# A gated GNN kernel: TensorE transposes of h and y replaced by VectorE block transposes and an exchange through DRAM

## The chip, the cores and the metric

The kernel runs as one program on one core of one Trainium2 chip. The metric is the device time of that program in microseconds (us). The engines named below are TensorE (PE, with its weight loads PEld), VectorE (DVE), ScalarE (ACT), GpSimd (POOL) and SyncE (SP, which here only issues DMAs). POOL issues DMAs too; POOL's go through queue q0, SP's through queue q1, and both feed the same 16 DMA engines.

## What is computed

There are 16 graphs of 1024 nodes with 128 features each, and an adjacency matrix `adj` of 1024 x 1024 zeros and ones for each. Two layers run one after the other, cut here to what matters:

```python
h = maximum(layernorm(x), 0)                       # y: per node, over the 128 features
for i in range(4):                                 # layer 0: gated
    m = einsum('bjn,bjd->bnd', adj, h @ weight[i])
    gx = m @ w_ih[i].T + b_ih[i];  gh = h @ w_hh[i].T + b_hh[i]
    r = sigmoid(xr + hr); z = sigmoid(xz + hz); n = tanh(xn + r * hn)
    h = (1 - z) * n + z * h
x = x + h * nodemask
h = maximum(layernorm(x), 0)
for i in range(4):                                 # layer 1: graph convolution with batch norm
    h = relu(einsum('bnm,bmc->bnc', adj, h @ W[i]) + b[i])
    h = batchnorm over all graphs and nodes (h)
out = x + h
```

## The kernel before

The program has two stages: a gated stage (layer 0, all graphs) and a convolution stage (layer 1, all graphs). A slower general path stands behind a flag that the exact path computes; it does not run here.

**Layout.** In the gated stage h lives transposed: features on the 128 partitions, nodes along the free axis, in halves of 512 nodes (`hf`). Gates and weights work on that layout. The aggregation needs the other one: nodes on the partitions, since it sums over source nodes. It takes h as a high part (rounded to fp32r) and a low part (the rest), so each aggregation multiplies two parts with the rows of `adj`, 32 matmuls of 512 columns (`aggregate_rows`, L521, matmul at L525).

**Turning by TensorE.** `split_step` (L741) makes the two parts. In layer 0 they come from `y`, which has nodes on the partitions already (`split_high`, `split_low`). In layers 1 to 3, `features_times` (L491) transposes h on TensorE, eight blocks of 128 x 128 into PSUM (L498, tile `hw_g`); ACT copies the high part out (L502) and DVE subtracts it for the low part (L503). Two more turns are on TensorE: `turn` (L639) turns y into the first h of a graph (L647, tile `pt_in`, copied out by ACT at L648), and `tail_norm` (L651) turns the last h back to nodes (L657, tile `pt_x`), which DVE adds to x (L660) before it takes the sums of the next layer norm (L609, L610). A nested function `rest` (L675) applies that norm on ACT (L625) and stores y for the convolution stage.

**Two streams and half-steps.** Stream A takes the even graphs and stream B the odd ones. `half_step(one, two)` (L856) lets stream `two` compute its gates (`gate_step`, L781, twice: for each half, six fp32 matmuls at L790, sigmoid, two DVE operations, tanh, sigmoid, three DVE operations) while stream `one` splits its h and then aggregates. The main loop (L997) calls it with the streams in turn, 60 times. Eight half-steps, a cycle, take a pair of graphs through the four layers. In the text they are numbered HS0 to HS7: in an even one A aggregates layer 0, 1, 2, 3 in turn (HS0, HS2, HS4, HS6) and B computes gates; in an odd one the roles are exchanged. B's gates of layer i run while A aggregates layer i+1.

After the aggregation ACT copies its two PSUM halves to `m` (L770); the next half-step's gates need h first (`g_r<-h`, one matmul) and then `m` (`g_r<-m`). The four gate results have one PSUM bank each (`g_r`, `g_hn`, `g_xn`, `g_z`), so the matmuls of the second half wait until ACT and DVE have read those of the first.

**Beside that** each graph needs, in the gated stage:
- its rows copied from the input to a scratch in DRAM (`copy_rows`, L572, eight DMAs of POOL), and loaded from there (`load_rows`, L577, eight DMAs of SP, called from `take` at the end of the stream's last gates);
- a check of the rows' low bits by DVE (`look`, L585), four rows at a time (`look_on`, L838);
- its rows cast to bf16 by POOL (L594) and turned by a DMA transpose of SP (L595), eight of each in one half-step (`transpose_rows`, L591), through two buffers; POOL then stores the turned matrix to `adjT_d`, laid out partition first, for the convolution stage;
- x of the graph two further on loaded and normed (`ahead`, L817): loaded by POOL when the stream is in layer 1, normed as a whole in layer 2, and turned on TensorE in layer 3.

**What sets the order.** In the start-up phase the order of all five engines is the program's own (`manual_schedule(engines=every)`). In the main loop only POOL's and SP's is (L995); PE, DVE and ACT are ordered by the framework's planner, which moves operations about, with a few `issue_after` fences (`behind`, L683). All engines execute their own instructions strictly in order. The convolution stage is ordered by the planner.

**The convolution stage** loads the turned matrices, 2-byte, in eight pieces of 256 KB for every graph and layer (`load_adjT`, L1018), widens them on DVE and ACT (L1026, L1028) and aggregates with the same L525. Odd graphs use the one large buffer (`block`), even graphs eight small ones (`packed`, tag `half`).

The functions that the change touches:

Of the kernel before, what the change touches and what calls it, by code (L numbers as in the profile page):

```python
# [16 lines left out]
P = 128  # L17
# [324 lines left out]
def exact_path(  # L342
# [42 lines left out]
    adjT_d = [dram.tile([P, NB, N], BF16, tag=f"adjT{b}", name=f"adjT_d{b}") for b in range(B)]  # L385
# [148 lines left out]
    with ExitStack() as st:  # L534
# [37 lines left out]
        def copy_rows(b):  # L572
            raws[b] = rawd.tile([N, N], F32, tag="raw", name=f"raw{b}")
            for j in range(NB):
                nc.gpsimd.dma_start(raws[b][j * P : (j + 1) * P, :], adj[b][j * P : (j + 1) * P, :])
# [8 lines left out]

        def look(b, row, j, part=0):  # L585
# [5 lines left out]
        def transpose_rows(b, row, j, adjT):  # L591

            t = work.tile([P, N], BF16, tag="half1", name=f"half{b}_{j}", bufs=2)
            nc.gpsimd.tensor_copy(t, row.bitcast(F32))  # L594
            nc.sync.dma_start_transpose(adjT[:, :, j * P : (j + 1) * P], t)  # L595

        def norm(xt, y, name):

            norm_apply(xt, y, norm_stats(xt, name))
# [39 lines left out]
        def turn(y, name, hT=None, func=AF.Copy):  # L639

            if hT is None:
                hT = work.tile([P, N], F32, tag="h", name=f"h_{name}", bufs=7)
# [8 lines left out]
        def tail_norm(b, xt, hT):  # L651

            for hf in range(NH):
                pt = tmp(f"pt_x{b}_{hf}")
                for q in range(BH):
                    k = hf * BH + q
                    nc.tensor.transpose(pt[:, q * P : (q + 1) * P], hT[:, k * P : (k + 1) * P], ident)  # L657
                for q in range(BH):
                    k = hf * BH + q
                    nc.vector.scalar_tensor_tensor(  # L660
                        xt[:, k, :],
                        pt[:, q * P : (q + 1) * P],
                        maskT[:, b * NB + k : b * NB + k + 1],
                        xt[:, k, :],
                        ALU.mult,
                        ALU.add,
                    )
# [13 lines left out]
        written = [True]  # L681

        def behind(*inss):  # L683

            es = ExitStack()
            for ins in () if written[0] else inss:
                es.enter_context(tc.issue_after(ins.ins))
            return es

        class Stream:  # L690


            def __init__(self, first):
                self.b, self.i, self.rest, self.tag = first, 0, None, "AB"[first % 2]
                self.opened = None
# [31 lines left out]
            def prepare(self, b, xt):  # L727
# [568 lines left out]
```

## Time and profile before

| what | value |
|---|---|
| time, median of 3 runs | 1842.16 us (1841.27 to 1842.33) |
| the profiled execution's own time | 1840.61 us |
| its span in the trace | 1838.8 us |
| PE busy | 1821.5 us, 99% of the span |
| DVE busy | 1225.6 us, 67% |
| ACT busy | 1035.8 us, 56% |
| POOL busy | 285.0 us, 15% |
| clock granted to TensorE | 0.999 of full speed |
| moved by DMA | 381 MB, 207 GB/s on average |

The gated stage fills the first 1,200 us or so and the convolution stage the rest. The page gives, for each engine, the time in which it executed something; a group line gives a line of the kernel, the engine, what is written from what, the count, the busy time, the mean duration of one in ns, and the idle time of the engine just ahead of the group's instructions with what ended it. In a table of windows each row is one stretch of time and gives the busy time of each engine in it. Matmuls overlap in the pipeline, so the durations of single matmuls add to more than the time they take; distances from one start to the next are the better measure.

### The profile page before, as it was taken

Reading aid. Unit: us, or ns where it says so; the run is one execution under the profiler, and the core shown is the slowest. Engines: PE = TensorE matmul, PEld = TensorE weight load, DVE = VectorE, ACT = ScalarE, POOL = GpSimd, SP = SyncE. Lnnn points to the kernel's source line nnn. Section 1 sums busy time; section 2 is a strip of 40 time slices with the busy share of each in tenths; the row PEclk is TensorE's granted clock in tenths of the full one; section 3 lists DMA queues with packets and bytes.
Section 4 is the critical chain, followed back from the end, with each engine's and each line's share of the span. In section 5 each row is a group of like instructions: output and inputs, shape, how many; then the busy total and the mean of one; then the engine's idle time right before and its main releaser. Section 6 shows DMA issues by size and latency. Waiting matters only on the chain.

```text
span 1838.8 us, 21960 instructions
## 1 busy us (share of the span) xinstructions
PE 1821.5 (99%) x7326; PEld 1254.2 (68%) x7326; DVE 1225.6 (67%) x2244; ACT 1035.8 (56%) x1577; POOL 285.0 (15%) x378
## 2 busy tenths in 40 slices
PE   9999999999999999999999999999999999999997
PEld 6566666656566666666565666667778888888886
DVE  7656667567666766766766757676666666666665
ACT  5544454553545554445355353467777767767764
POOL 4131320230231042023023013011100000000011
PEclk9999999999999999999999999999999999999999
DMA  7189775575486386567557546349876676767676
GB/s 264 39 247 317 209 229 195 162 206 192 159 233 180 126 233 178 196 172 217 218 159 206 178 145 172 103 159 332 291 248 228 212 256 204 257 209 260 210 249 242
DMA packets 256280, 381.21 MB, mean 207 GB/s; under 512 B 149932, under 2 KB 155856, under 8 KB 252320
## 3 DMA queue, kind: packets, MB, share of 16 engines
q1 hardware_dynamic: 237968, 245.95, 44.2%
q0 software_dynamic: 17664, 133.53, 20.4%
q8 instruction: 59, 0.97, 0.2%
q14 instruction: 61, 0.50, 0.1%
q10 hardware_dynamic: 528, 0.26, 0.0%
HBM read 287.39 MB, written 117.44 MB: 220 GB/s over the span
## 4 chain that ended last, share of the span: by engine, by line
PE 94%; DVE 2%; ACT 2%; issue 1%; DMA 1%; SPq 0%; POOL 0%; DVEq 0%; ACTq 0%; POOLq 0%
PE pm L525 24%; PE pc_m L525 12%; PE g_r L790 11%; PE g_z L790 11%; PE pc_g_r L525 6%; PE pc_g_z L525 6%; PE g_hn L790 6%; PE g_xn L790 6%; PE hw_c L500 4%; PE hw_g L498 2%; PE pw_g_hn L1096 1%; PE pw_g_xn L1096 1%; PE pt_in L647 1%; PE pt_x L657 1%; PE pc_g_r L510 1%
## 5 line engine op out<-in xcount | busy, mean ns | idle before, releaser
L525 PE MATMUL pm<-row,ghw 128*128 128x512 f32 x2048 | 515.6, 406 | 0.1
L525 PEld LDWEIGHTS pm<-row,ghw 128*128 128x128 f32 x2048 | 383.2, 188 | 112.6 <-issue 36.9
L525 PE MATMUL pc_m<-wide,chw 128*128 128x512 f32 x1024 | 246.0, 395 | 0.0
L525 PEld LDWEIGHTS pc_m<-wide,chw 128*128 128x128 f32 x1024 | 190.5, 188 | 42.3 <-issue 4.3
L807 ACT ACTIVATE r<-r,vecs 128x512 f32<-128x512 f32 x128 | 92.3, 721 | 216.8 <-DVE r L804 216.8
L525 PE MATMUL pc_g_r<-wide,chw 128*128 128x512 f32 x464 | 187.0, 403 | 0.3 <-ACT chw L502 0.3
L525 PE MATMUL pc_g_z<-wide,chw 128*128 128x512 f32 x464 | 180.9, 390 | 0.0
L594 POOL CAST half<-row 128x1024 bf16<-128x1024 f32 x128 | 139.7, 1108 | 250.9 <-DMA adjT<-half 169.6
L1028 DVE CAST wide<-packed 128x1024 fp32r<-128x1024 bf16 x160 | 110.0, 692 | 74.5 <-PE pc_m L525 56.4
L1028 DVE CAST wide<-block 128x1024 fp32r<-128x1024 bf16 x160 | 110.2, 691 | 73.2 <-PE pc_g_z L525 40.2
L503 DVE TENSOR_TENSOR ghw<-hw_g,ghw 128x512 fp32r<-128x512 f32 x96 | 62.0, 686 | 129.7 <-ACT ghw L502 129.5
L1026 ACT CAST wide<-block 128x1024 fp32r<-128x1024 bf16 x96 | 100.6, 1048 | 59.3 <-PE pc_m L525 34.3
L803 DVE SCALAR_TENSOR_TENSOR r<-g_hn,vecs,r 128x512 f32<-128x512 f32 x128 | 95.4, 745 | 56.8 <-ACT r L802 31.3
L1026 ACT CAST wide<-packed 128x1024 fp32r<-128x1024 bf16 x96 | 100.7, 1049 | 55.6 <-PE pc_g_z L525 23.7
L790 PE MATMUL g_r<-m,w_mT 128*128 128x512 f32 x256 | 130.7, 592 | 0.0
L790 PE MATMUL g_z<-m,w_mT 128*128 128x512 f32 x256 | 130.7, 592 | 0.0
L790 PE MATMUL g_xn<-m,w_mT 128*128 128x512 f32 x256 | 130.7, 592 | 0.0
L589 DVE TENSOR_REDUCE low<-row 128x1 f32<-128x1024 uint16 x112 | 128.6, 1210 | 0.0
L808 ACT ACTIVATE z<-g_z,brz 128x512 f32<-128x512 f32 x128 | 87.1, 680 | 71.0 <-PE g_z L790 71.0
L770 ACT COPY m<-pm 128x512 f32<-128x512 f32 x128 | 68.8, 586 | 101.3 <-PE pm L525 101.2
L802 ACT ACTIVATE r<-g_r,brz 128x512 f32<-128x512 f32 x128 | 87.7, 685 | 60.3 <-PE g_r L790 59.5
L810 DVE TENSOR_TENSOR h<-h,r 128x512 f32<-128x512 f32 x96 | 74.6, 777 | 62.4 <-ACT r L807 62.4
(176 smaller groups left out, 2764.0 us busy)
## 6 DMA issues: line engine op xcount, KB each, us to landing
packed<-adjT_d SPq DMA_DIRECT2D x256, 256.0 KB, 5.9
block<-adjT_d SPq DMA_DIRECT2D x256, 256.0 KB, 5.4
raw<-in_adj_dram POOLq DMA_DIRECT2D x112, 512.0 KB, 11.6
row<-raw SPq DMA_DIRECT2D x112, 512.0 KB, 5.8
adjT_d<-adjT POOLq DMA_DIRECT2D x16, 2048.0 KB, 7.9
xmid_d<-x POOLq DMA_DIRECT2D x16, 512.0 KB, 4.8
y<-ymid_d POOLq DMA_DIRECT2D x16, 512.0 KB, 5.1
ymid_d<-y_mid POOLq DMA_DIRECT2D x15, 512.0 KB, 3.0
```

The source lines that it names most:

```text
L500: nc.tensor.matmul(pt[:, q * P : (q + 1) * P], src, w, start=True, stop=True)
L525: nc.tensor.matmul(pm[hf], hw[s][:, j * P : (j + 1) * P], rows[j][:, hf * HALF : (hf + 1) * HALF], start=(j == 0 and s == 0), stop=(j == N ...
L589: nc.vector.tensor_reduce(low[:, k : k + 1], lows, axis=AX.X, op=ALU.max)
L594: nc.gpsimd.tensor_copy(t, row.bitcast(F32))
L790: nc.tensor.matmul(po, wT[:, i, g * C : (g + 1) * C], rhs, start=start, stop=stop)
L802: nc.scalar.activation(r, pr, AF.Sigmoid, bias=brz[:, 3 * i : 3 * i + 1])
L803: nc.vector.scalar_tensor_tensor(r, phn, b_hn(i), r, ALU.add, ALU.mult)
L807: nc.scalar.activation(r, r, AF.Tanh, bias=b_in(i))
L808: self.last_act = nc.scalar.activation(z, pz, AF.Sigmoid, bias=brz[:, 3 * i + 1 : 3 * i + 2])
L810: nc.vector.tensor_sub(ho, hin, r)
L1026: nc.scalar.copy(r, t)
L1028: nc.vector.tensor_copy(r, t)
```

## The change

Every turn of h and y in the main loop leaves TensorE. DVE transposes 32 x 32 blocks of a 128 x 512 half in one instruction, with the blocks written in an order that puts what belongs to the same destination partitions together. The 128 partitions are then exchanged in four groups of 32: SP stores the tile to a scratch in DRAM (`exchange_out`, one DMA of 256 KB with 2 KB rows) and loads it back into the same tile by four DMAs (`exchange_in`, 64 KB each, in pieces of 512 B). The result has nodes on the partitions in their own order and stays in the permuted order along the free axis; the readers use views (`nodes_of`, `four_ways`, `by_nodes`) with runs of 32 elements. Three kinds of turn go this way: h after every gate half (`gate_step`), y of the next graph (`turn_across`), and the last h of a graph, which `tail_norm` takes from the same exchanged tile. The first three splits, the turns of y of graphs 0 and 1 and the tails of graphs 14 and 15 stay on TensorE.

With it the main loop gets an order written out by hand for all five engines:
- the split (`split_part`) is put between the gates of the other stream: the ACT copy of the high part and the DVE subtraction stand ahead of the tanh of the same half, and read SBUF, not PSUM;
- the second half's load back, the turning of rows and all side work come after the gates, in fixed places (`beside_aggregation`): the tail of a graph comes half a step later than before, and the norm of x is spread over three layers;
- rows are loaded at the start of the half-step in which the stream computes its last gates (before: after them);
- casts, DMA transposes and row copies go four at a time over four half-steps (before: eight in one), and two of every four casts write to a tile of the `half` pool, which the exchange tiles use too;
- `adjT_d` is laid out block first, and even and odd graphs exchange their buffers in the convolution stage.

```diff
-    adjT_d = [dram.tile([P, NB, N], BF16, tag=f"adjT{b}", name=f"adjT_d{b}") for b in range(B)]
+    adjT_d = [dram.tile([NB, P, N], BF16, tag=f"adjT{b}", name=f"adjT_d{b}") for b in range(B)]
...
+        def exchange_out(t, name):
+            d = rawd.tile([P, HALF], F32, tag="cross", name=f"cross_{name}", bufs=6)
+            nc.sync.dma_start(d, t)
+            return d
+
+        def exchange_in(d, t):
+
+            src = d.rearrange("(t r) (s x) -> s r t x", t=4, s=4)
+            for s in range(4):
+                nc.sync.dma_start(t[s * 32 : (s + 1) * 32, :].rearrange("r (t x) -> r t x", t=4), src[s])
...
-            t = work.tile([P, N], BF16, tag="half1", name=f"half{b}_{j}", bufs=2)
+            if j % 4 < 2:
+                t = work.tile([P, N], BF16, tag="half1", name=f"half{b}_{j}", bufs=2)
+            else:
+                t = half_tile(f"half{b}_{j}")
             nc.gpsimd.tensor_copy(t, row.bitcast(F32))
             nc.sync.dma_start_transpose(adjT[:, :, j * P : (j + 1) * P], t)
...
+        def turn_across(y, name):
+
+            hT = work.tile([P, N], F32, tag="h", name=f"h_{name}", bufs=7)
             for hf in range(NH):
-                pt = tmp(f"pt_x{b}_{hf}")
+                cols = slice(hf * HALF, (hf + 1) * HALF)
+                t = half_tile(f"ty_{name}_{hf}").bitcast(F32)
+                nc.vector.transpose(
+                    t.rearrange("p (a k i) -> p k a i", a=4, i=32), y[:, cols].rearrange("p (k a c) -> p k a c", a=4, c=32)
+                )
+                exchange_in(exchange_out(t, f"{name}_{hf}"), hT[:, cols])
+            return hT
+
+        def by_nodes(cols):
+            return cols.rearrange("c (q k i) -> c k q i", q=4, i=32)
+
+        def four_ways(cols):
+            return cols.rearrange("p (k a c) -> p k a c", a=4, c=32)
+
+        def nodes_of(t):
+
+            return t.rearrange("p (a k c) -> p k a c", a=4, c=32)
...
+            def split_part(self, g):
+                if g == 0:
+                    self.hw = hw_tiles(self.b, f"ghw{self.b}_{self.i}")
+                if self.i == 0:
                     self.split_high(g)
                     self.split_low(g)
+                    return
+                hi, lo = (four_ways(t[:, g * HALF : (g + 1) * HALF]) for t in self.hw)
+                src = nodes_of(self.parts[g])
+                nc.scalar.copy(hi, src)
+                nc.vector.tensor_sub(lo, src, hi.bitcast(F32))
...
+                if self.goes_across():
+                    t = half_tile(f"th{nm}").bitcast(F32)
+                    nc.vector.transpose(t.rearrange("p (q k c) -> p k q c", q=4, c=32), four_ways(ho))
+                    self.outs.append((exchange_out(t, f"h{nm}"), t))
+                if hf == 0:
+                    self.exchange()
...
+        def turn_rows():
+
+            for b, row, j in waiting_rows[:4]:
+                if j == 0:
+                    adjTs[b] = turned_tile(f"adjT{b}")
+                transpose_rows(b, row, j, adjTs[b])
+                if j == NB - 1:
+                    nc.gpsimd.dma_start(adjT_d[b].rearrange("k p n -> p k n"), adjTs[b])
+            del waiting_rows[:4]
+            for dst, src in copies[:4]:
+                nc.gpsimd.dma_start(dst, src)
+            del copies[:4]
+
+        def beside_aggregation(one, two):
+
+            if one.b + 2 < B and one.i == 2:
+                one.next_apply()
+            if two.ends:
+                two.ends.pop(0)()
+            if one.ends:
+                one.ends.pop(0)()
+            if two.b + 2 < B and two.i == 2:
+                two.next_sums()
+            if one.b + 2 < B and one.i == 3:
+                one.next_turn()
+            one.look_on()
+
         def half_step(one, two, gated=None, halfway=None):
 
-            if one.i > 0:
+            if one.i == 1:
+                one.give_rows()
+            if two.i == L - 1 and two.b + 2 < B:
+                two.next_rows = load_rows(two.b + 2)
+            by_turns = one.i > 0 and not one.parts
+            if by_turns:
                 one.split_step()
-            two.gate_step(0)
-            two.gate_step(1)
+            for hf in range(NH):
+                two.gate_step(hf, None if by_turns else lambda: one.split_part(hf))
             if gated:
                 gated()
-            if one.i == 0:
-                one.split_step()
+            two.exchange()
+            if two.i == 1:
+                two.ahead()
+            turn_rows()
+            beside_aggregation(one, two)
             one.agg_step(0)
...
-        with tc.manual_schedule(engines={mybir.EngineType.Pool, mybir.EngineType.SP}):
-            written[0] = False
+        with tc.manual_schedule(engines=every):
+            stage_two.append(True)
             for s in range(2, B // 2 * L):
                 half_step(sa, sb)
                 half_step(sb, sa)
+        with tc.manual_schedule(engines={mybir.EngineType.Pool, mybir.EngineType.SP}):
             sb.gate_step(0)
             sb.gate_step(1)
...
-        block = turned_tile(f"block{b}_{i}") if b % 2 else None
+        block = None if b % 2 else turned_tile(f"block{b}_{i}")
```

In the code `between` runs after a half's two first DVE operations and ahead of its tanh, and `self.parts` holds the exchanged tiles of a stream's newest h. `look_on` now looks at rows in layers 1 and 3 of stream A and 2 and 3 of stream B.

## The prediction

> **What bounds the kernel now.** I read the busy shares first, then one cycle of eight half-steps in windows, then PE's order of time, then the groups that the change touches, and last the DMAs.
>
> The page's busy line and its DMA slices:
>
> ```profile
> PE 1821.5 (99%) x7326; PEld 1254.2 (68%) x7326; DVE 1225.6 (67%) x2244; ACT 1035.8 (56%) x1577; POOL 285.0 (15%) x378
> ...
> DMA  7189775575486386567557546349876676767676
> ```
>
> PE has no room; DVE and ACT have a third and more. Windows of one cycle, about a half-step each (length, then busy time of PE, PEld, DVE, ACT, POOL, then clock, DMA share, GB/s):
>
> ```profile
> 591.10:609.50 18.40, 18.40 (x65) 11.39 (x64) 14.00 (x20) 7.13 (x13) 0.00 (x0) 1.00 0.59 210
> 609.50:628.00 18.50, 18.50 (x65) 11.40 (x64) 12.22 (x40) 10.83 (x21) 1.47 (x2) 1.00 0.42 167
> 628.00:646.40 18.40, 18.40 (x65) 11.39 (x64) 10.78 (x35) 11.06 (x20) 2.69 (x4) 1.00 0.17 57
> 646.40:665.00 18.60, 18.60 (x65) 11.40 (x64) 13.88 (x16) 7.46 (x12) 6.50 (x11) 1.00 1.01 315
> 665.00:683.40 18.40, 18.40 (x65) 11.39 (x64) 13.28 (x31) 8.02 (x15) 8.85 (x11) 1.00 0.62 124
> 683.40:704.00 20.60, 20.60 (x69) 12.08 (x68) 11.05 (x30) 13.20 (x25) 5.63 (x9) 1.00 0.95 307
> 704.00:722.50 18.50, 18.50 (x71) 11.69 (x70) 13.54 (x17) 10.16 (x18) 5.51 (x6) 1.00 0.69 182
> 722.50:741.00 18.50, 18.50 (x72) 11.85 (x71) 13.10 (x17) 6.65 (x12) 0.00 (x0) 1.00 0.39 138
> ```
>
> PE is full in every window. DVE sums to 101.9 us of 149.9, ACT to 74.5, the DMA shares to 89.6 us. So in this stage whatever leaves PE shortens the cycle, until something else is late. PE's order of time shows what leaves (start, length, instruction):
>
> ```profile
> 637.64 7.85 PE L525 MATMUL pm<-row,ghw 128*128 128x512 f32 x32
> 645.33 1.03 PE L498 MATMUL hw_g<-ident,h 128*128 128x128 f32 x8
> 646.20 1.02 PE L790 MATMUL g_r<-h_in,w_hhT 128*128 128x512 f32 x2
> 647.06 1.02 PE L790 MATMUL g_r<-m,w_mT 128*128 128x512 f32 x2
> ```
>
> From start to start eight transposes take 646.20 - 645.33 = 0.87 us and a gate matmul 0.86. A half-step without turns is 12 x 0.86 = 10.3 us of gates and 7.3 of aggregation, 17.6 us; eight are 141.
>
> **1. Turns taken off PE.** Counts from the groups:
>
> ```profile
> L498 PE MATMUL hw_g<-ident,h 128*128 128x128 f32 x384 | 50.0, 272 | 0.2 <-ACT w_mT L488 0.2
> L657 PE MATMUL pt_x<-ident,h 128*128 128x128 f32 x128 | 16.7, 272 | 0.0
> L647 PE MATMUL pt_in<-ident,y_in 128*128 128x128 f32 x128 | 16.6, 272 | 0.0
> ```
>
> Three splits of 48, two tails and two turns of y stay: 384 - 24, 128 - 16, 128 - 16, so 584 transposes go, at 0.87/8 each: **-63.5 us**, all on the path.
>
> **2. DVE transposes.** 118 for h (59 layers of graphs, two halves) and 28 for y, 20 in a cycle. No row shows one. Nearest from below: the widening cast at L1028, 1024 columns in 0.69 us, so 0.35 for 512; from above: the low-bit check at L589, 1.21 us for 1024 elements. I take 0.7, what a 128x512 DVE operation takes undisturbed (L811: 0.69). DVE's cycle becomes 102 + 14 = 116 us of 141 (126 at the upper bound): it fits, so 0.
>
> The Trainium skill, "VectorE: DVE Perf Modes", "The three transpose paths", gives 311 ns for 128x128 bf16 on VectorE and advises TensorE for a full 128x128 turn where PSUM will do, which speaks against this change. Its figure would estimate 1.24 us here and 127 us of DVE in a cycle; the price it puts on TensorE, 390 ns, is not what this trace shows as PE's cost, 0.109 us in a chain of eight. Its advice would forbid the move; the windows, with PE full and DVE not, allow it.
>
> **3. Split and tail from SBUF.** ACT's copy of the high part goes from 0.60 us (PSUM source, L502) to 0.63 (SBUF source, L753), DVE's subtraction from 0.69 to 0.70 (L757). The 28 copies of `h_in` (0.60 us) leave ACT. Hidden, since both engines have slack.
>
> **4. Order, and the copies of `m`.** The eight transposes also covered ACT's copy of `m`. Now only one gate matmul (0.86 us) does; the copy takes 0.59. With ACT free it just fits. In four half-steps of eight ACT is inside a norm (table load 1.28, root 0.30, eight activations 3.2 together), begun after the last sigmoid, about 11.2 us into the half-step, with DVE's two small operations now behind the new transpose (about 13.6): it ends at 17 to 18 us, against an aggregation that ends at 17.6. I take 0.3 us a time, 4 x 7 cycles: **+8 us** (bounds 0 and 1.2 us a time, 34).
>
> **5. The exchange.** SP stores 256 KB, waits, issues four loads, and the next half-step's split needs them. Clock from the start of a half-step: first half's sigmoid 2.6, DVE to 4.3, tanh 5, sigmoid z 5.9, three DVE operations 7.4, transpose 8.1. In the next half-step ACT wants the tile at 17.6 + 2.5 = 20.1. Late by L, it holds the tanh and the sigmoid z behind it on ACT, which PE needs to reuse bank `g_z` at 26.1 in the second half; copy, tanh and sigmoid are 2.0, so PE feels it only from 24 on: 16 us after the transpose. For the second half it is the low part, needed in mid-aggregation, with 17 us. DMA rows (issue to landing; the last line is that of L595):
>
> ```profile
> ymid_d<-y_mid POOLq DMA_DIRECT2D x15, 512.0 KB, 3.0
> x<-in_x_dram POOLq DMA_DIRECT2D x14, 512.0 KB, 6.3
> DMA to landing us min/median/max: 3.0/3.2/12.7
> ```
>
> The store: 3 us. The loads, 512 B pieces as in x: four issues at 0.32 us (SP's row of L581) and 3.7 us (a lone 256 KB of x at the start). Together 8 us, half of what is allowed. From above: while eight row copies keep the DMA engines full (646 to 662 us, share 1.0) a DMA transpose took 11.2 us to land; two in series would be 22. The copies now come four at a time, and only HS2 to HS5 have any, so I take 8 to 14 us and no wait of PE. Volume: the packet records have 84 ns for 2 KB and 27 ns for 512 B, so (128 x 84 + 512 x 27)/16 = 1.5 us an exchange, 31 a cycle: 120 of 141, 85%. In the gated stage the exchanges share q1 with the DMA transposes, 1.23 us of SP each, now four a half-step and behind the exchange.
>
> The skill's "DMA: Bandwidth & Descriptors", "Anatomy of one DMA", puts a fixed 2.0 us on each DMA and its rules say transfers under 64 KB are mostly overhead. By it store and loads would be 2.6 and about 2.6 in series, some 5 us, even less than the rows give; contention is what it leaves out.
>
> **6. Rows loaded early.** Eight loads (10 us of DMA at 159 ns per 4 KB) now stand in q1 ahead of the stores of layer 3's h. Those are wanted only by the tail, after the next gates, 13 us later; y's exchanges have two half-steps. Cover: that distance. 0.
>
> **7. POOL casts beside DVE.** DVE operations with two SBUF sources stretch while POOL casts:
>
> ```profile
> 652.88 2.73 DVE L810 TENSOR_TENSOR h<-h_in,r 128x512 f32<-128x512 f32 x1 [1.95 <-ACT r L807]
> 653.04 2.03 POOL L594 CAST half<-row 128x1024 bf16<-128x1024 f32 x2
> ```
>
> 0.69 became 2.73. The casts now come in fours and the subtraction joins the exposed operations; whether the transpose does is not shown. Per cycle the stretching costs some 5 us of DVE now; at most all 17 us of casts. Inside DVE's room; 0, with up to 1.5 us of PE in HS2 to HS5 as the upper bound, 42 us.
>
> **8. Strided gate operands.** In layer 0 of 14 graphs, 84 matmuls read h and write PSUM in runs of 32. No row has that; the nearest, the last transposes' strided weight load, takes 211 ns against 141. I take 0 (whole runs of 128 B) and 36 us as the upper end (half as slow again).
>
> **9. `adjT_d` and buffers.** A graph's store becomes 2 KB pieces, 672 ns for eight against 622 for 16 KB: 0.4 us of DMA a graph, hidden; the convolution stage moves the same 2 KB packets under a full PE. 0.
>
> **Sum** against the profiled 1840.6 (span 1838.8 and 1.8 around it): 1840.6 - 63.5 + 8 = 1785. The median shown is 1.6 above that execution: **1787 us**.
>
> **Rivals.**
> - *Covers are thin.* Terms 4, 7 and 8 bite together, 0.6 to 1.5 us in half of the 60 half-steps: 20 to 45 us. For it: the planner had moved PE's h-matmuls ahead of the `m` ones where ACT was late (683.1 to 685.7 us); a fixed order can't. Against: ACT is only half busy. About 1815.
> - *The exchange is late* (slower). Place: HS2 to HS5, 28 of them. At 22 us PE waits 22 - 16 = 6 each: 28 x 6 = 168 - 63.5, so 1947. It decides from 63.5/28 = 2.3 us beyond the limit, an exchange of 18 us. For it: the share of 1.0 beside the copies, the 11.2 us landing. Against: copies halved per half-step.
> - *DVE becomes the bound* (slower). From (149.9 - 102)/20 = 2.4 us a transpose; at 3 us a cycle is 162: 7 x 12 = +84, so 1926. Against: no 512-column row is over 0.75 undisturbed.
> - *No net change*: the covers lose exactly what PE gains, 1842.
>
> **Chances.** Forecast 0.53 (own range 1774 to 1800), thin covers 0.21, late exchange 0.15, DVE 0.07, no change 0.04. Within 0.2% (3.7 us, about what a measurement tells from nothing): 0.04; faster 0.74; slower 0.22. The range starts at 1772, a few us under the bare sum, and reaches past thin covers and no change into a mildly late exchange, 1860.
>
> **What would show it.** Right: `pt_in` and `hw_g` gone from PE's order, half-steps at 17.6 us, DVE transposes near 0.7 us, ACT's copy of the high part waiting for no DMA. Wrong: PE idle behind `m` (term 4) or behind ACT's sigmoid (5); transposes over 1.2 us (2); gate matmuls `h_in` above 0.86 apart (8). A landing of the four loads more than 16 us after the DVE transpose would make the whole forecast wrong.

## The result, and the profile after

The changed kernel takes **2049.23 us** (median, 2038.67 to 2051.97) against 1841.72 (1840.73 to 1842.33) for the kernel before beside it: 1.1117 times as long, 95% interval 1.1077 to 1.1156. The forecast was 1787 us, so 262 us have to be found. The profiled execution took 2050.01 us, its span is 2047.8.

The page's span, busy line, and its slices of clock and DMA:

```profile
span 2047.8 us, 22360 instructions
...
PE 1838.1 (90%) x6742; PEld 1211.6 (59%) x6742; DVE 1358.5 (66%) x2390; ACT 1022.6 (50%) x1551; POOL 296.3 (14%) x378
...
PEclk9989899988999998898999989999999999999999
DMA  6376686767669666866866786678987666666566
```

The 584 turns are gone (7326 - 6742), yet PE is busy *longer* than before (1838.1 against 1821.5 us) and idle for 209.7 us besides (before: 17.3). No other engine is full. The clock, 0.999 before, has dips all through the gated stage. So PE waits, and after waiting it runs slower.

Windows of one cycle, cut where an aggregation starts, so that a row holds the aggregation of one half-step and the gates of the next (length, busy time of PE, PEld, DVE, ACT, POOL, clock, DMA share, GB/s):

```profile
545.50:569.90 24.40, 18.68 (x58) 10.35 (x56) 15.92 (x41) 6.95 (x12) 0.92 (x1) 1.00 0.56 185
569.90:599.70 29.80, 22.13 (x55) 10.84 (x56) 13.45 (x39) 11.12 (x20) 2.36 (x3) 0.89 0.67 235
599.70:617.30 17.60, 17.60 (x57) 10.57 (x56) 15.22 (x19) 12.11 (x21) 8.42 (x11) 1.00 0.66 176
617.30:636.10 18.80, 17.83 (x57) 10.48 (x56) 13.90 (x30) 5.45 (x9) 3.93 (x3) 1.00 0.78 169
636.10:655.50 19.40, 17.89 (x57) 10.48 (x56) 13.80 (x35) 12.01 (x21) 8.75 (x13) 1.00 0.92 282
655.50:688.00 32.50, 21.12 (x57) 12.14 (x56) 18.29 (x23) 12.51 (x22) 6.80 (x7) 0.84 0.80 194
688.00:706.30 18.30, 17.91 (x59) 10.52 (x57) 13.08 (x18) 5.46 (x9) 1.44 (x3) 1.00 0.83 280
706.30:723.90 17.60, 17.60 (x59) 10.59 (x57) 16.55 (x23) 6.68 (x11) 0.00 (x0) 1.00 0.71 258
```

Two rows are the forecast itself: 17.60 us, PE full. The loss sits in three of eight: 24.4 and 29.8 us where the pair of graphs changes, and 32.5 in the middle of the cycle. Over 8 x 17.6 = 140.8 us, this cycle loses 37.6; 33.9 of them are in those three rows (6.8 + 12.2 + 14.9). The bad rows are not the ones with the highest DMA share.

What PE waited for, who made it wait, and what those engines waited for (total us, times, longest; groups of waits over the whole span):

```profile
ACT ghw L775 <- DMA th<-cross_h: 280.2, 49, 15.7
...
DVE x L696 <- DMA th<-cross_h: 154.7, 28, 13.6
...
PE g_hn L821 <- DVE r L834: 70.3, 14, 8.5
...
PE g_z L821 <- ACT z L839: 35.4, 12, 12.0
...
PE pm L525 <- ACT ghw L775: 32.8, 6, 8.7
PE g_r L821 <- ACT m L797: 29.9, 14, 4.0
PE pm L525 <- DMA row<-raw: 16.8, 14, 2.9
```

The last five are 185.2 of PE's 209.7 idle us. Three of them (138.5) end with an ACT or DVE instruction that itself stood behind `th<-cross_h`, the load back of an exchange: ACT's copy of the high part (L775) and the tail's addition to x (L696). Followed back wait by wait, all but 2.4 of these 138.5 us have such a wait just ahead of them. The exchange is late. The queue that issues it (the same view for SP) shows how:

```profile
SPq L594 <- DMA cross_h<-th: 490.8, 118, 17.0
...
SPq L594 <- DMA cross_in<-ty_in: 65.3, 28, 3.9
```

All 118 exchanges of h make SP wait at the load for the store's landing, 4.2 us on average, 17.0 at the most, and the 28 of y do the same; SP issues nothing else meanwhile. SP's order of time around the change of the pair (start, length, instruction; `cross_in` is an exchange of y):

```profile
556.27 0.38 SPq L587 DMA_DIRECT2D cross_in<-ty_in  x1
...
560.23 0.38 SPq L587 DMA_DIRECT2D cross_in<-ty_in  x1
...
565.98 4.15 SPq L581 DMA_DIRECT2D row<-raw  x8
570.23 0.39 SPq L587 DMA_DIRECT2D cross_h<-th  x1
579.93 1.83 SPq L594 DMA_DIRECT2D th<-cross_h  x4
581.87 0.57 SPq L587 DMA_DIRECT2D cross_h<-th  x1
585.17 2.15 SPq L594 DMA_DIRECT2D th<-cross_h  x4
587.42 0.38 SPq L587 DMA_DIRECT2D cross_h<-th  x1
589.59 1.73 SPq L594 DMA_DIRECT2D th<-cross_h  x4
```

Three exchanges are seen in a row behind eight row loads of 512 KB, and each begins only when the store before it has landed. The tile of the store at 570.23 had been transposed by 544.53; the exchanges of earlier tiles, two of them of y, and the issue of the rows filled the 25.7 us between. Its store then took 9.7 us (570.23 to 579.93) behind the 4 MB of rows, and its loads landed at 584.74: 40.2 us from transpose to landing, for a tile that an undisturbed exchange delivers in 5.3 to 6.0 us (store 2.0, four issues 1.3, loads 2.0). Over all 118, worked out from the starts and landings of each instruction: mean 19.2 us, median 16.6, longest 42. Of the mean, 9.5 us pass *before SP issues the store*, 4.8 until it lands, 1.4 with four issues and 3.4 until the loads land.

The other engines at the same place, in order of time:

```profile
584.91 1.14 DVE L696 SCALAR_TENSOR_TENSOR x<-th,maskT,x 128x128 f32<-128x128 f32 x4 [12.02 <-DMA th<-cross_h]
...
593.21 0.73 DVE L834 SCALAR_TENSOR_TENSOR r<-g_hn,vecs,r 128x512 f32<-128x512 f32 x1
...
593.99 2.08 PE L821 MATMUL g_hn<-h_in,w_hhT 128*128 128x512 f32 x2 [6.66 <-DVE r L834]
```

The tail's addition is side work, but DVE runs in order: the sequence of instructions on every engine is the same here as in the run with small packets below, where the waits are others. It holds DVE for 12.02 us, and for 2.92 more at its second half; the tail's sums follow; the gate operation L834 behind it comes at 593.21, and PE has been idle for 6.66 us. Then comes a second loss, in narrow windows of the same stretch (columns as before):

```profile
590.00:593.00 3.00, 0.00 (x0) 0.00 (x0) 2.76 (x16) 0.00 (x0) 0.90 (x1) 0.92 0.57 177
593.00:596.00 3.00, 2.01 (x3) 0.98 (x4) 2.31 (x6) 1.37 (x3) 0.00 (x0) 0.50 0.51 173
596.00:599.00 3.00, 3.00 (x5) 1.21 (x4) 2.83 (x5) 1.56 (x3) 0.00 (x0) 0.50 0.31 87
599.00:602.00 3.00, 3.00 (x11) 1.94 (x10) 2.60 (x5) 1.74 (x4) 0.00 (x0) 0.94 0.25 94
```

The granted clock is 0.50 for some 6.8 us (6.0 in the middle rows; 0.08 x 3/0.5 and 0.06 x 3/0.5 at the ends). PE works in 5.4 of them, and the pairs of gate matmuls that start at 595.86 and 597.57 take 1.7 us each to the next start, in place of 0.86. Counted over the trace's whole record of the clock, PE was busy for 114.6 us at 0.50, which is some 57 us of work lost.

In the middle of the cycle, SP once more, then POOL, ACT and PE (each in order of time):

```profile
644.95 1.02 SPq L587 DMA_DIRECT2D cross_h<-th  x1
657.86 1.90 SPq L594 DMA_DIRECT2D th<-cross_h  x4
659.87 9.68 SPq L609 DMA_TRANSPOSE adjT<-half  x4
669.64 0.53 SPq L587 DMA_DIRECT2D cross_h<-th  x1
672.02 1.73 SPq L594 DMA_DIRECT2D th<-cross_h  x4
```

```profile
644.17 1.97 POOL L911 DMA_DIRECT2D raw<-in_adj_dram  x4
...
650.07 1.45 POOL L911 DMA_DIRECT2D raw<-in_adj_dram  x3
652.64 0.49 POOL L911 DMA_DIRECT2D raw<-in_adj_dram  x1 [1.12 <-DMA adjT_d<-adjT]
```

```profile
667.76 0.62 ACT L775 CAST ghw<-th 128x512 fp32r<-128x512 f32 x1 [14.19 <-DMA th<-cross_h]
```

```profile
668.43 7.00 PE L525 MATMUL pm<-row,ghw 128*128 128x512 f32 x16 [8.65 <-ACT ghw L775]
```

POOL had waited 20.49 us at the store of `adjT_d` (until 643.26) and then issued eight row copies between 644.17 and 653.1, two half-steps' worth together. The store at 644.95 took 12.9 us beside them and its loads 8.3 more after the last of them was issued; four DMA transposes held SP for 9.68 where 5.4 is usual, and ACT waited 14.19 us for the tile. PE stood 8.65 us in the middle of an aggregation, and the clock was 0.51 from 664 to 672.

### The profile page after: what moved, and what is told of

It reads as the page before. It is cut to its first block, busy times and chain, and to the rows that moved or that the text cites. A ratio compares the mean times of both kernels' runs of the same rounds, so it can differ in the third digit from the quotient of the medians.

```text
span 2047.8 us, 22360 instructions
## 1 busy us (share of the span) xinstructions
PE 1838.1 (90%) x6742; PEld 1211.6 (59%) x6742; DVE 1358.5 (66%) x2390; ACT 1022.6 (50%) x1551; POOL 296.3 (14%) x378
## 5 line engine op out<-in xcount | busy, mean ns | idle before, releaser
L525 PE MATMUL pm<-row,ghw 128*128 128x512 f32 x2048 | 535.1, 416 | 53.2 <-ACT ghw L775 32.8
L525 PEld LDWEIGHTS pm<-row,ghw 128*128 128x128 f32 x2048 | 392.8, 194 | 189.2 <-DMA row<-raw 38.3
L775 ACT CAST ghw<-th 128x512 fp32r<-128x512 f32 x90 | 55.3, 614 | 287.7 <-DMA th<-cross_h 280.2
L608 POOL CAST half<-row 128x1024 bf16<-128x1024 f32 x128 | 144.2, 1166 | 142.0 <-DMA adjT<-half 142.0
L776 DVE TENSOR_TENSOR ghw<-th,ghw 128x512 fp32r<-128x512 f32 x90 | 69.8, 775 | 140.0 <-ACT ghw L775 139.8
L821 PE MATMUL g_r<-m,w_mT 128*128 128x512 f32 x256 | 134.2, 606 | 29.9 <-ACT m L797 29.9
L834 DVE SCALAR_TENSOR_TENSOR r<-g_hn,vecs,r 128x512 f32<-128x512 f32 x128 | 93.2, 728 | 83.9 <-ACT r L833 42.5
L821 PE MATMUL g_xn<-m,w_mT 128*128 128x512 f32 x256 | 142.7, 641 | 0.0
L821 PE MATMUL g_z<-m,w_mT 128*128 128x512 f32 x256 | 135.3, 611 | 0.0
L821 PE MATMUL g_z<-h,w_hhT 128*128 128x512 f32 x192 | 103.4, 621 | 35.4 <-ACT z L839 35.4
L696 DVE SCALAR_TENSOR_TENSOR x<-th,maskT,x 128x128 f32<-128x128 f32 x112 | 31.9, 347 | 154.7 <-DMA th<-cross_h 154.7
## 6 DMA issues: line engine op xcount, KB each, us to landing
raw<-in_adj_dram POOLq DMA_DIRECT2D x112, 512.0 KB, 12.2
```

Of the source, the lines that this page charges most:

```text
L525: nc.tensor.matmul(pm[hf], hw[s][:, j * P : (j + 1) * P], rows[j][:, hf * HALF : (hf + 1) * HALF], start=(j == 0 and s == 0), stop=(j == N ...
L696: nc.vector.scalar_tensor_tensor(xk, pt[:, q, :, :], mask, xk, ALU.mult, ALU.add)
L775: nc.scalar.copy(hi, src)
L776: nc.vector.tensor_sub(lo, src, hi.bitcast(F32))
L821: nc.tensor.matmul(po, wT[:, i, g * C : (g + 1) * C], rhs, start=start, stop=stop)
L834: nc.vector.scalar_tensor_tensor(r, phn, b_hn(i), r, ALU.add, ALU.mult)
```

## The experiments

Each edit is to the changed kernel, unless it says otherwise. "Half-step" is from one start of an aggregation to the next.

**The bare order without transfers.** Every exchange DMA is left out (and y is transposed straight into its first h).

```diff
         def exchange_out(t, name):
-            d = rawd.tile([P, HALF], F32, tag="cross", ...)
-            nc.sync.dma_start(d, t)
-            return d
+            return t
         def exchange_in(d, t):
-            src = ...
-            for s in range(4): nc.sync.dma_start(...)
+            return
```

> Leaves out all DMAs of the exchange: the tile that VectorE transposed is used as it is, and y is transposed straight into its first h (values no longer the reference's). Hand-written order, VectorE transposes, early row loads and all else stay. Theory Q (the exchange comes late because it stands in line, on SyncE and in its DMA queue): 1775 to 1800 us, half-steps of 17.6 us, TensorE waiting under 30 us. Rival H (the order written by hand and the VectorE work are what costs): still above 1842, some 1900 to 2000 us.

Measured: 1803.52 us, 0.9797 (0.9768 to 0.9825). From the second cycle on, five to seven half-steps of eight are at 17.6 us; the others, 18 to 22 us, lie in its middle. So the transfers are worth 2049 - 1804 = 246 us, and the gates, copies, turns and side work of the new order cost about 16 over the forecast.

**Stores alone, and loads alone.** In the first, the four loads are left out and y is transposed straight into its first h, as above; the 28 stores of y stay as well as the 118 of h. In the second, all loads read one scratch tile that is written once, and no store is issued.

```diff
 # stores only
-            for s in range(4): nc.sync.dma_start(t[...], src[s])
+            return
 # loads only
-            d = rawd.tile(...); nc.sync.dma_start(d, t); return d
+            return const_d
```

> Of the exchange only the stores of h stay (118 of 256 KB); the loads back are left out and the unexchanged tile is used, y is transposed in place (values no longer the reference's). SyncE then never waits for a store to land. Theory Q (what costs is the chain on SyncE: wait for the store, then loads, then whatever stands behind): close to the run without transfers (1803), 1800 to 1830 us. Rival V (the bytes on the DMA engines): half of the lost 246 us comes back, 1900 to 1940 us.

> Of the exchange only the loads stay, all from one scratch tile that is written once; no store is issued, so no load waits for one (values no longer the reference's). The split still waits for its loads. Theory Q: 1805 to 1860 us, above the stores alone since the loads are in the split's way and stand behind row loads and copies in their queue. Rival V: 1900 to 1950 us. If line order in the DMA queue alone (not SyncE's waits) makes the exchange late, it stays above 1950.

Measured: stores alone 1802.19 us (0.9791, 0.9763 to 0.9820), as without any transfer; loads alone 1844.88 (1.0022, 1.0008 to 1.0036), 41 to 43 more. Together they cost 246. Each half of the traffic by itself is cheap, and six times the sum of the halves appears when a load has to wait for its store in SP's line. With loads alone the loss is mostly in one place, 20 to 29 us in the sixth half-step of a cycle. That the coupling is the wait, and not the traffic of both, is what the later runs on other queues test.

**Row loads off SP.** GpSimd issues them.

```diff
-                nc.sync.dma_start(t.bitcast(F32), raws[b][...])
+                nc.gpsimd.dma_start(t.bitcast(F32), raws[b][...])
```

> The eight row loads of a graph are issued by GpSimd in place of SyncE, at the same point of the program; the same bytes move. Theory Q: the exchange of layer 3 no longer stands behind them, so VectorE's wait for the tail's tile (155 us in the changed kernel) falls under 40 and the time by 80 to 120, to 1930 to 1970 us. Rival B (the DMA engines are simply too full): the bytes are the same, so within 15 us of 2049.

Measured: 2002.16 us (1.0876, 1.0802 to 1.0949), 47 less, where 80 to 120 were expected. The waits for exchanged tiles:

```profile
ACT ghw L775 <- DMA th<-cross_h: 286.3, 49, 13.7
...
DVE x L696 <- DMA th<-cross_h: 47.6, 21, 3.3
```

The tail's wait falls from 154.7 to 47.6 us, so most of it came from the rows ahead of layer 3's exchange; ACT's does not fall (280.2 before the edit), and half-steps of 27 to 34 us remain in the middle. Rows are one of several causes.

**No copies.** Only those for graphs 2 and 3 are made, and later graphs use those rows again.

```diff
-                if self.b + 2 < B:
+                if self.b < 2:
                     copies.extend(copy_rows(self.b + 2))
```

> The rows of graphs 2 and 3 alone are copied to the DRAM scratch and loaded again for every later pair (the later graphs get wrong adjacency matrices); 96 of 112 copies are left out. If the copies' burst is what delays the exchange in the middle of a cycle, ScalarE's wait for the exchanged tile (280 us) halves and the time falls by 70 to 110, to 1940 to 1980 us; the tail's wait (155 us) stays. If line order on SyncE alone matters, less than 25 us of gain.

Measured: 1935.77 us (1.0515, 1.0477 to 1.0554), 113 less; ACT's wait for tiles falls from 280.2 to 106.9 us. The 32 us half-step is gone (18 to 23 are left there) and the 29 us one at the change of the pair stays: the two jams have different causes, copies in the middle, rows at the change.

**Tail by TensorE.** Layer 3's h is not exchanged; the tail is turned on PE as before the change.

```diff
-                return stage_two and not (self.b >= B - 2 and self.i == L - 1)
+                return stage_two and self.i < L - 1
```

> The last h of a graph is turned by TensorE again, as before the change, and isn't exchanged: 14 of 59 exchanges of h and the tail's wait go, 112 transposes (12 us) come back. Theory Q: 2049 + 12 - 90 to 110, so 1950 to 1975 us. Rival (the tail's wait only fills time in which VectorE is idle anyway): 2049 to 2061 us.

Measured: 1940.90 us (1.0543, 1.0508 to 1.0578), 108 less and better than expected, though it gives PE 112 turns back (12 us at 0.109). The second row of the cycle falls from 29.8 to between 19 and 21 us. It takes away a quarter of the exchanges, the ones behind the rows, and with them the DVE wait.

**Packet size.** The scratch's row pitch becomes 4352 bytes, so that a copy goes in pieces of 4 KB. Alone, and with the row loads on GpSimd.

```diff
-            raws[b] = rawd.tile([N, N], F32, ...)
+            raws[b] = rawd.tile([N, N + 64], F32, ...)[:, :N]
```

> The scratch that rows are copied to gets rows of 4352 bytes in place of 4096, so that a copy can no longer go in 32 KB packets but goes in 4 KB ones; bytes, places and order stay. Theory P (the DMA engines alternate packet by packet between the queues, so an exchange with 8 and 32 packets on each engine stands behind as many 1.45 us packets): stores and loads of the exchange beside copies fall from 10 to 18 us to 3 to 6, ScalarE's wait for the tile (280 us) under 150, time 1950 to 1990 us. Theory V (volume: the engines are full while rows are copied, whatever the packets): 2035 to 2060 us.

> Small packets and row loads issued by GpSimd together. If the two delays are separate (line order at the pair's change, packets in the middle), the gains add: 47 us from the row loads alone and 60 to 100 from the packets, so 1900 to 1945 us. If the row loads only moved the jam elsewhere, above 1970.

Measured: 2024.20 us (1.0995, 1.0963 to 1.1027) and 1983.27 (1.0773, 1.0676 to 1.0870): 25 less alone, 19 less on top of the rows on GpSimd. The longest store fell from 18.3 to 11.3 us, the longest load from 17.7 to 11.0, but ACT's wait for tiles only from 280.2 to 259.2. Together with the row loads on GpSimd the time stays above 1970, the bound at which the loads were said only to move the jam: ACT waits 278.4 us for tiles there. My theory that the copies' large packets hold up the exchange was mostly wrong: 25 us of the 113 that the copies cost.

**Rows straight from the input.** GpSimd's DMA loads each row from `adj`, converting to fp32r on the way; no copy is made.

```diff
-                nc.sync.dma_start(t.bitcast(F32), raws[b][j * P : (j + 1) * P, :])
+                nc.gpsimd.dma_start(t, adj[b][j * P : (j + 1) * P, :])
...
-                if self.b + 2 < B:
-                    copies.extend(copy_rows(self.b + 2))
```

> Rows come straight from the input to their tiles by GpSimd DMAs that write fp32r, and the copies to a scratch are dropped; the result stays the reference's. It takes away both the copies (113 us alone) and the rows from SyncE (47 us alone). If they add: about 1885 us, and down to 1830 if the rest of the jam goes with them. If a DMA that writes fp32r is slow, TensorE waits for rows and it is above 2000.

Measured: 1875.01 us (1.0185, 1.0155 to 1.0214), 174 less: close to the sum of the two single steps (47 + 113). Both jams are gone; half-steps of 19 to 23 us remain, with ACT still waiting 107.2 us for tiles.

**The same loads in the kernel before.** To see whether the missing copies are a gain by themselves.

> The kernel before, with its rows loaded straight from the input by GpSimd and no copies. TensorE is full there, so dropping the copies should give nothing by itself: 1836 to 1846 us. If the copies cost the kernel before something as well, below 1836, and that part of the gain is not the exchange's.

Measured: 1864.22 us (1.0126, 1.0111 to 1.0142), 23 *slower* than the kernel before. PE there waits 9.6 us, and its weight loads 29.9, for rows that now land 9.5 us after their issue. So the 174 us are not a gain of a cheaper way to load rows; they come from what rows and copies did to the exchange, the rows in SP's line and the copies beside it.

**Exchange of y on GpSimd, alone and with the gates reordered.** On top of the rows from the input; the reordering puts the gate's second matmul on h (`g_hn`) ahead of the first on `m`.

```diff
-                exchange_in(exchange_out(t, f"{name}_{hf}"), hT[:, cols])
+                exchange_in(exchange_out(t, f"{name}_{hf}", nc.gpsimd, "y"), hT[:, cols], nc.gpsimd)
 # the second run only
                 part(pr, w_hhT, 0, hin, True, False)
-                part(pr, w_mT, 0, m, False, True)
                 if not self.opened:
                     part(phn, w_hhT, 2, hin, True, True)
+                part(pr, w_mT, 0, m, False, True)
```

> Rows straight from the input and the exchange of y on GpSimd, with the gates' matmuls in the old order (the kernel with both edits: 1816 us, the one with neither: 1875). If y's exchange on SyncE made the exchange of h late, most of the 59 us is here: 1820 to 1840. If the wait for m was the larger part, 1845 to 1870.

> On top of the rows that come straight from the input (1875 us): the exchange of y is issued by GpSimd, so SyncE has only that of h and the DMA transposes, and the gates' second matmul is one that needs h and not m, which gives ScalarE 0.86 us more for its copy of m. TensorE's wait for m (42 us there) falls under 15, the tail's wait (36 us) under 15: 1830 to 1860 us. If the waits for m are long because ScalarE itself is late by more than 1 us, 1860 to 1875.

Measured: 1821.63 us (0.9896, 0.9878 to 0.9914) and 1816.15 (0.9867, 0.9839 to 0.9896). Moving 28 exchanges to another queue, with the same bytes, is worth 53 us; the order of the gates 5.5. The second time is below its expected range, though PE's wait for `m` stays above the 15 that was named. Waits of the reordered one:

```profile
PE g_r L821 <- ACT m L797: 21.2, 9, 3.1
ACT ghw L775 <- DMA th<-cross_h: 6.5, 6, 2.4
```

ACT's wait for tiles has gone from 280.2 to 6.5 us. SP still waits 316.4 us for stores, and little of it reaches PE. The means over the 118 exchanges of h, worked out as above, show where the time went (us):

| run | transpose to store | store | loads, from the last issue | all |
|---|---|---|---|---|
| changed kernel | 9.5 | 4.8 | 3.4 | 19.2 |
| row loads off SP | 7.0 | 4.4 | 3.7 | 16.6 |
| no copies | 6.9 | 3.6 | 2.8 | 14.8 |
| rows straight from the input | 4.7 | 3.2 | 3.3 | 12.7 |
| and y on GpSimd | 0.4 | 3.3 | 3.4 | 8.6 |

Between the last two rows the bytes are the same and the transfers take as long; only the wait in SP's line goes, and 53 us with it. This is the test that the two half-traffic runs left open, made without the copies: what is left of the loss there was the line, and not the traffic. What the copies add by crowding the DMA engines and what by lengthening the line is not separated.

**The norm spread, and a store moved.** Two more steps, each on top of the last: the eight activations of a norm are spread over two half-steps, with x loaded a round later; then POOL issues the store of `adjT_d` one half-step later, when the transposes that it needs have landed.

```diff
-            norm_blocks(xt, y, nt, range(NB))
+            pend.extend(lambda k=k: block(k) for k in range(NB))
+            run_late(4 if spread else NB)
...
                 if j == NB - 1:
-                    nc.gpsimd.dma_start(adjT_d[b]..., adjTs[b])
+                    stores.append(b)
```

> In addition each norm's eight ScalarE activations are spread over two half-steps (four after the gates, two after the first half's last sigmoid, the rest after the next gates), and x is loaded one round later, when its buffer is free. If ScalarE's norm is what holds up m: 10 to 25 us below the kernel before it, 1810 to 1845 us. Otherwise within 5 us of it.

> On top of the spread norm (1811 us): GpSimd issues the store of a graph's turned matrix one half-step later, behind the load of x, so that its wait for the last DMA transposes no longer holds up x and the casts. If the loss that is left in the fifth half-step of a cycle (20 to 23.6 us in place of 17.6) comes from x arriving late and from four casts that stall a small VectorE operation for 3.9 us, half of it goes: 1785 to 1800 us. If the casts alone do it, 1803 to 1811.

Measured: 1810.96 us (0.9839, 0.9810 to 0.9868) and **1789.86 us** (1787.88 to 1791.47; 0.9722, 0.9709 to 0.9735). What was left in the first of the two, around its slow half-step of 20 to 24 us (order of time):

```profile
672.07 0.89 POOL L921 DMA_DIRECT2D adjT_d<-adjT  x1 [17.77 <-DMA cross_h<-th]
...
684.80 0.29 DVE L619 BATCH_NORM_STATS2 st_in<-x 128x6 f32<-128x128 f32 x1 [5.67 <-DMA x<-in_x_dram]
...
688.75 2.08 PE L834 MATMUL g_hn<-h,w_hhT 128*128 128x512 f32 x2 [2.86 <-DVE r L847]
```

The same pattern over again, one queue further: POOL stands for 17.77 us at the store of `adjT_d` and so issues x only at 674.23, 73.6 us into its cycle; DVE waits for x with a side operation, the gate operation stands behind it, and PE waits. With the store a half-step later x is issued 58.1 us into the same cycle, and neither this wait of PE nor that of DVE is left in any cycle. What does remain in the last kernel is this (order of time):

```profile
666.51 3.98 POOL L608 CAST half<-row 128x1024 bf16<-128x1024 f32 x4
666.96 3.56 DVE L631 SCALAR_TENSOR_TENSOR ms_in<-mv_in,rs_in 128x8 f32<-128x8 f32 x1
```

An operation on eight columns, 0.17 us in the median, takes 3.56, as long as the POOL casts beside it, and ACT begins the norm's activations 4.58 us late; PE feels little of that, by way of `m`: 0.49 us here, and up to 1.5 in other cycles.

The last kernel's busy line, and what its PE waited for:

```profile
PE 1758.4 (98%) x6742; PEld 1195.3 (67%) x6742; DVE 1360.8 (76%) x2390; ACT 1021.9 (57%) x1551; POOL 378.3 (21%) x518
```

```profile
PE g_hn L834 <- DVE r L847: 5.5, 2, 4.3
PE g_r L834 <- ACT m L810: 5.5, 6, 1.5
```

Its cycles take 141.4 to 142.4 us: every half-step 17.6 but one of 18.3 to 19.4. It has all the exchanges of the changed kernel and is 2.8% faster than the kernel before.

## Why the prediction was wrong, by its own steps

With the last kernel as the measure of what PE has to do (1758.4 us busy, same matmuls), the changed kernel's span splits into three numbers: idle time 209.7 against 17.3 before, **+192.4**; the same work taking longer, 1838.1 - 1758.4 = **+79.7**; work taken away, 1821.5 - 1758.4 = **-63.1**. They sum to +209.0, the difference of the spans (2047.8 - 1838.8). Of the 79.7, the clock explains some 56: PE was busy for 114.6 us at 0.50, against 3.4 in the last kernel. The other 24 are busy time at full clock around the waits; the first row of the cycle above has 18.68 us at clock 1.00 for work that takes 17.60.

**Right.**
- *Turns off PE (term 1):* -63.5 forecast, -63.1 found; half-steps of 17.60 us with PE full. The time forecast, 1787, was reached within 3 us by the last kernel, which has the same turns and exchanges but other queues for them, no row copies and other side work; that it comes so close is partly chance.
- *DVE transposes (term 2):* 0.7 us taken, 0.711 measured:

```profile
L851 DVE STREAM_TRANSPOSE th<-h 128x512 f32<-128x512 f32 x118 | 84.0, 711 | 6.2
```

The estimate of 1.24 us scaled up the Trainium skill's 311 ns for a 128x128 bf16 turn on VectorE ("VectorE: DVE Perf Modes", "The three transpose paths"); for this form the measurement decides against it. The same page's advice to turn 128x128 on TensorE ("Rules for kernel authors") would have spoken against a move that, with the exchange repaired, gains 2.8%. The rival in which DVE becomes the bound is refuted: 120.2 us of DVE in the cycle of 178.4, and as much DVE work (1360.8 us) in the last kernel, whose cycles take 142.
- *Split from SBUF (3), strided gate operands (8):* ACT's copy 0.614 us (0.63 forecast), DVE's subtraction 0.775 (0.70); the gate matmuls on the strided h of layer 0 start 0.86 us apart (580.30, 581.16, 582.02), as the others do.
- *Layout of `adjT_d` (9):* no wait of PE leads to it by its layout. Its store did matter, as the instruction that POOL stands behind.

**Wrong: term 5, "The exchange".** Its durations were good: "Together 8 us" against 5.3 to 6.0 undisturbed. (The section of the Trainium skill from which it estimated some 5 us, "Anatomy of one DMA" in "DMA: Bandwidth & Descriptors", is on DMAs that GpSimd issues; these are SP's.) The limit of 16 us agrees with the runs as far as they go: in the last two kernels of the series the slowest exchange took 15.6 and 15.0 us, and no wait of PE led to a tile. The failing sentence is "I take 8 to 14 us and no wait of PE". It priced store, issue and loads and left out the time *until the store is issued*, 9.5 us on average and 33.7 at the most, twice the store itself. The prediction knew that SP stores, waits and loads in line, and gave that line no occupancy: five issues and a wait of 4.2 us for each of the 16 exchanges of h in a cycle, four of y, 16 row loads and 16 DMA transposes at 1.23 us. My upper bound, "two in series would be 22", was from landings alone; 42 occurred, and the mean of 19.2 is itself past the 16 that the prediction had named as its sign of being wrong. One of its sums is off as well, without consequence: the DMA shares of its eight windows make 91.5 us of DMA and not 89.6, so 122 of 141 with the exchanges.

**Wrong: term 6, "Cover: that distance. 0."** The rows do stand ahead of layer 3's stores as it says, but the 13 us of distance are gone before the first store is issued: 25.7 us passed from transpose to store, the last 4.15 of them with issuing the rows and 9.7 with two exchanges of y, for which the step had no price. Then come 9.7 us of that store landing behind 4 MB, and another exchange in series, with its own wait. The tail is not wanted early, but DVE runs in order, and the gates stand behind it. The step asked when the tile is needed and not what is queued behind the instruction that needs it. Taking the rows off SP is worth 47 us alone.

**Terms 4 and 7, sizes.** PE waited 29.9 us for `m`, inside the bounds (0 to 34), over the 8 taken; in the last kernel, with the order of the gates changed, 5.5. The stretched operations (7) are real, up to 3.72 us for one of 0.17 in the last kernel, but PE's waits for `m` that can come from them are 5.5 us there, near the 0 that was taken.

**The rival "the exchange is late"** is what happened, and 0.15 was too little for it. Its place was partly right: the large waits are in the gates of HS1 and HS2 and in the aggregation of HS5, so two of the three lie in the range it named. Its mechanism, landings that are slow beside copies, is that of HS5; HS1 and HS2 are the line. Its price of 168 us of waits compares with 192 found. It lacked the clock: some 56 us that no term had. The Trainium skill ("TensorE: Matmul & The Clock Gate", "What's actually happening") says that the clock halves after an idle window of about 3.4 us and comes back after a busy one of that length. The trace agrees on the length: in its record of the clock each of the 28 dips ahead of the run's end lasts 3.41 us or two or three times that (6.83 around 594, 10.24 around 668). But an idle stretch need not be that long: a dip followed all 15 stretches over 4 us, and also 13 of the 22 between 2.0 and 3.8 us, the one of 2.60 us at 676 not among them. A late-tile rival has to be priced as the wait plus what the clock takes after it.

**Where the 262 us went, step by step:** rows and copies out of the exchange's way 174, y's exchange off SP 53, gate order 5.5, norm 5, the store moved 21; together 259. The order in which the steps are made matters, so the single numbers are not properties of the steps: rows alone are 47 on the changed kernel, copies alone 113.

**Open.** Why a store takes 10 to 18 us beside eight copies is not settled: packet size is 25 of the 113 us, and neither the size of the copies nor the queues' shares were varied by themselves. Nor is it settled why the loads alone cost 42 us, mostly in one half-step; in that run SP's longest DMA transposes, 10 to 12 us each, are issued while seven or eight row copies are in flight, and the loads stand behind them.

## What to carry to other kernels

Price a DMA that waits for another DMA on the queue's own line, not as a transfer: write down for each queue, in order, every issue and every wait of a stage, and ask when the *last* of them is issued; then give each chain of dependent transfers a queue that nothing bulky shares. Side work that needs a late tile delays everything behind it on an in-order engine, however idle that engine is on average. And a stall of TensorE can cost clock after it: every idle stretch over 4 us did here, and over half of those from 2.0 to 3.8 us; 192 us of added idle time brought some 56 us of lost clock.

## What the hardware showed that I had not expected

- Around idle stretches of 6.66 and 8.65 us, TensorE's granted clock was 0.50 for 6.83 and 10.24 us, of which it worked 5.4 and 5.9; stretches of 2.0 us were also followed by 3.41 us at 0.50, though one of 3.79 us was not.
- DVE transposes 128x512 fp32 in 32 x 32 blocks, with a permuted output, in 0.711 us, about what an elementwise operation of that size takes undisturbed (0.69 at L835).
- A 256 KB store to DRAM and its load back by 512-byte pieces take 5.3 to 6.0 us undisturbed (2.0 + 1.3 + 2.0), and 40 us from transpose to landing when the line and the queue are full.
- Issuing a DMA transpose on SP took 1.29 us in the median and up to 11.0: the longest fell beside row copies, so the issuing engine can lose time too, and not only the landing.
- A DVE operation on 128x8 elements with two SBUF sources took 3.56 us in place of 0.17 while POOL made four casts.
- A DMA that converts fp32 to fp32r on the way lands 512 KB in 7.8 us (9.5 in the kernel before), where the load from a copied scratch had 6.9 in the changed kernel, so the copy can be saved where nothing waits for it closely.
